# Index work of a graph layer by blocks of 96 edge tiles, early feature loads, and ten gather buffers for twelve

## The chip, the cores and the metric

One core of a Trainium2 chip. The metric is the device time of one execution in microseconds, the median of the runs shown; the profile is of one execution more, with its own time. TensorE is called PE, VectorE DVE, ScalarE ACT, GpSimd POOL; SP issues transfers only.

## What is computed

One message-passing layer on a graph of N = 12,500 nodes with 160 features (64 scalars and 32 vectors of three) and 400,000 edges sorted by destination:

```
h   = relu(layernorm(x))
y0  = h[:, :64] @ W_l1_0 * attr / 8          y1 = (32 vectors of h) x W_l1_1 * attr / sqrt(32)
w   = silu(e16 @ fc_W1 / 4) @ fc_W2 / 8      # 192 weights for each edge
mid = products of w, of y0[src], y1[src] and of the four numbers e4 of the edge   # 96 + 3 x 96
z   = segment sum of mid over dst / sqrt(10)
out = x + sin(pi/8) * (h x W_sc) * attr + cos(pi/8) * (z x W_l2) * attr
```

All in float32. The sum over destinations is a matmul with a selection matrix: 128 edges at a time, a one-hot matrix of the destination inside a window of 32 nodes.

## The kernel before

**Edges.** The 400,000 edges are 3,125 tiles of 128. Four tiles are a batch (782 batches), three tiles a window (`WT`) of at most 32 destination nodes, four windows (12 tiles, three batches) a group (261 groups), eight groups a block of 96 tiles (24 batches; `EG * TG`), 33 blocks.

**Node stage** (lines 268 to 412). The 98 node tiles, and 40 further tiles of rows that are gathered in advance, go through DVE (statistics, centering: L326 to L328), PE (transposes L347 and L348, linear maps L363 and L364), ACT (out of PSUM: L354, L375) and back to DRAM: `y_d` holds the mapped features of all nodes (L378), `yr_d` those of ten batches of edges (L380), called "made" batches: batch 12, 24, ... 120. For these POOL gathers 40 tiles of `x` and 40 columns of `attr` (L306, L309) early on. DVE also adds the skip path into `acc` (L386). After the 16th of the node stage's steps `first_nodes` converts `dst` to float in `drel` (L131), takes the least node of each window (`neg`, L134), and POOL reduces that over the partitions into `negb` (L138).

**`relate`** (L143 to L183) makes the index work on all edges at once: the node tile of each group (`first`, `tile_i`), the places of its four windows (`at`), the limits of each window (`lim`), then over all 3,125 columns: `drel` minus the window's first node (L174), whether an edge falls outside (`over`, L175), whether any does (`far`, L177, then a matmul and `far_i`, L183), and `drel` pushed out of range for these (L179). Such edges would be worked off in a slow loop at the end, which runs zero or one times after `far_i`.

**Edge stage** (L438 to L655). For each batch, `load` (L466 to L475) brings the edge features `xe` by SP, once for eight batches, and the rows of `y_d` by four indirect gathers on POOL into one of the buffers of pool `yg` (L475); a made batch comes from `yr_d` with one transfer on SP (L472). `e4_load` (L515) brings the four numbers of each edge for a block into `raw`, `e4_join` (L522, L523) puts them beside `drel` into `ev` on ACT. `hidden` and `activate` (L484, L489) are the first layer of the edge network, `weigh` (L506) the second, `scale` (L423, L424) multiplies by `e4` and appends the indices, `select` (L537, L539) and `products` (L429 to L436) make the operands on DVE, `sums` (L557 to L564) multiplies and takes the window's sums out, `turn`, `linear`, `add`, `accumulate` (L572 to L604) map a group and add it into `acc`.

**What sets the order.** On PE, ACT and DVE the order inside each `manual_schedule` is written out by hand; between such blocks, and on SP and POOL, a scheduler places instructions, and each engine then works its queue in order. Memory comes from pools: a tile of a later pool waits until the tiles that lie in its place are done with. `load(b + AHEAD)` stands `AHEAD` = 10 batches ahead in the written order; the pool `yg` has 12 buffers, and a gather into a buffer waits for the `products` that read it before. `xe` and `raw` belong to pool `ld`, opened after `relate`.

Of the kernel before, what the change touches and what calls it, by code (L numbers as in the profile page):

```python
# [10 lines left out]
F32 = mybir.dt.float32  # L11
I32 = mybir.dt.int32
AF = mybir.ActivationFunctionType
ALU = mybir.AluOpType
AX = mybir.AxisListType
PSUM = bass.MemoryType.PSUM
DRAM = bass.MemoryType.DRAM

P = 128
# [11 lines left out]
WT = 3  # L31
GW = 4
TG = WT * GW
EG = 8
# [11 lines left out]
def kernel(  # L46
# [19 lines left out]
    nc = tc.nc  # L66
    N = x.shape[0]
    NT = attr.shape[1]
    TP = src.shape[1]
    T = n_edges // P  # L70
    assert n_edges % P == 0 and TP % BT == 0 and NT == (N + P - 1) // P and NT >= 2
    NWIN = (T + WT - 1) // WT
    NG = (NWIN + GW - 1) // GW
    NB = (T + GT - 1) // GT
    ZR = (NT + 1) * P
# [8 lines left out]
    const = ctx.enter_context(tc.tile_pool(name="const", bufs=1))  # L84
# [31 lines left out]
    drel = const.tile([P, TP], F32, name="drel")  # L116
# [2 lines left out]
    far_i = const.tile([1, 1], I32, name="far_i")  # L119
    full = T // WT  # L120

    ygp = ctx.enter_context(tc.tile_pool(name="yg", bufs=12))
    before = ctx.enter_context(ExitStack())
    ip = before.enter_context(tc.tile_pool(name="idx", bufs=1))
    dst_i = ip.tile([P, TP], I32, name="dst_i")
    neg = ip.tile([P, NG * GW], F32, name="neg")
    negb = ip.tile([P, NG * GW], F32, name="negb")

    def first_nodes():

# [6 lines left out]
            nc.vector.tensor_reduce(neg[:, full:NWIN], drel[:, full * WT:T], AX.X, ALU.min, negate=True)  # L137
        nc.gpsimd.partition_all_reduce(negb, neg, P, bass_isa.ReduceOp.max)  # L138

    def relate(rp, cnt):  # L140

        first = rp.tile([P, NG], F32, name="first")
        nc.vector.tensor_reduce(first, negb.rearrange("p (g w) -> p g w", w=GW), AX.X, ALU.max, negate=True)  # L143
        nc.vector.tensor_copy(tile_i, first)
        nc.vector.tensor_scalar(tile_i, tile_i, 7, None, ALU.arith_shift_right)
        nc.vector.tensor_copy(first, tile_i)
        nc.vector.tensor_scalar(first, first, float(NT - 2), None, ALU.min)
        for lo, i in FLOORS:
            nc.vector.tensor_scalar(first[:, lo:], first[:, lo:], float(i), None, ALU.max)
        nc.vector.tensor_copy(tile_i, first)  # L150

        nc.vector.tensor_scalar(first, first, -float(P), None, ALU.mult)
        off = rp.tile([P, NG * GW], F32, name="off")
        nc.vector.tensor_tensor(off.rearrange("p (g w) -> p g w", w=GW),
                                first.unsqueeze(2).to_broadcast([P, NG, GW]),
                                negb.rearrange("p (g w) -> p g w", w=GW), ALU.subtract)
        node_of = rp.tile([P, 1], F32, name="node_of")
        for w in range(GW):
            nc.vector.tensor_scalar(node_of[WN * w:WN * (w + 1), :], lane[WN * w:WN * (w + 1), :],
                                    -float(WN * w), None, ALU.add)  # L160
        for w in range(GW):
            r = slice(WN * w, WN * (w + 1))
            nc.vector.tensor_scalar(at[r, :], off[r, :].rearrange("p (g w) -> p w g", w=GW)[:, w, :],
                                    node_of[r, :], None, ALU.add)
        lim = rp.tile([P, NG * GW], F32, name="lim")
        nc.vector.tensor_scalar(lim, off, -1.0, float(2 * P), ALU.mult, ALU.add)
        nc.vector.tensor_scalar(lim, lim, float(WN), None, ALU.min)
        nc.vector.scalar_tensor_tensor(lim, off, 0.0, lim, op0=ALU.is_ge, op1=ALU.mult)
        over = rp.tile([P, TP], F32, name="over")
        for lo, n, t in ((0, full, WT), (full, NWIN - full, T - full * WT)):  # L170
            if n:
                v = drel[:, lo * WT:lo * WT + n * t].rearrange("p (s t) -> p s t", t=t)
                o = over[:, lo * WT:lo * WT + n * t].rearrange("p (s t) -> p s t", t=t)
                nc.vector.tensor_tensor(v, v, negb[:, lo:lo + n].unsqueeze(2).to_broadcast([P, n, t]), ALU.add)  # L174
                nc.vector.tensor_tensor(o, v, lim[:, lo:lo + n].unsqueeze(2).to_broadcast([P, n, t]), ALU.is_ge)  # L175
        far = rp.tile([P, 1], F32, name="far")
        nc.vector.tensor_reduce(far, over[:, :T], AX.X, ALU.max)  # L177

        nc.vector.scalar_tensor_tensor(drel[:, :T], over[:, :T], float(ZR), drel[:, :T], op0=ALU.mult, op1=ALU.add)  # L179
        if T < TP:  # L180
            nc.vector.memset(drel[:, T:], 0.0)
        nc.tensor.matmul(cnt, far, one, start=True, stop=True)
        nc.vector.tensor_scalar(far_i, cnt, 1.0, None, ALU.min)  # L183

# [48 lines left out]
    def edge_weights():  # L233
        nc.vector.tensor_scalar(w2, w2, 1.0 / math.sqrt(FC_H), None, ALU.mult)
        f = C_X / math.sqrt(10.0 * (M0 + M1))
        nc.vector.tensor_scalar(wc, wor, f, None, ALU.mult)
        nc.vector.tensor_scalar(wc[M0:M0 + M1, 0, 0:M0], wc[M0:M0 + M1, 0, 0:M0], 1.0 / math.sqrt(3.0), None, ALU.mult)
        nc.vector.tensor_scalar(wo[:, :, 0:M0], wor[:, :, 0:M0], f, None, ALU.mult)
        nc.vector.tensor_scalar(wo[M0:M0 + M1, 0, 0:M0], wo[M0:M0 + M1, 0, 0:M0], 1.0 / math.sqrt(3.0), None, ALU.mult)
        nc.vector.tensor_scalar(wo[:, :, M0:].rearrange("p k (u c) -> p k c u", c=3),  # L240
                                wor[:, :, M0:].rearrange("p k (c u) -> p k c u", c=3), f, None, ALU.mult)
# [27 lines left out]
    with (  # L269
# [119 lines left out]
        with tc.manual_schedule(engines=engines):  # L389
# [14 lines left out]
            for q in range(len(steps) + 5):  # L404
# [4 lines left out]
                for stage, lag in ((scales, 1), (leave, 4), (out_of_psum, 2), (turn_rows, 1), (map_rows, 3), (center, 0),  # L409
                                   (add_s, 5)):  # L410
                    if 0 <= q - lag <= last:
                        stage(q - lag)
    with tc.tile_pool(name="rel", bufs=1) as rp, tc.tile_pool(name="rel_p", bufs=1, space=PSUM) as rpp:
        with tc.manual_schedule(engines=engines):
            edge_weights()
            relate(rp, rpp.tile([1, 1], F32, name="cnt"))
    before.close()


    def scale(pw, ev, n):  # L420
# [17 lines left out]
    with (  # L438
        tc.tile_pool(name="selp", bufs=3) as selp,
        tc.tile_pool(name="prod", bufs=3) as prod,  # L440
        tc.tile_pool(name="ld", bufs=2) as ld,
        tc.tile_pool(name="ev", bufs=2) as evp,
        tc.tile_pool(name="hid", bufs=4) as hid,
        tc.tile_pool(name="post", bufs=2) as post,
# [47 lines left out]
        def hidden_pair(s):  # L492

            pair = [i for i in (s, s + 1) if 2 * i < NB]
            for i, ph in [(i, hidden(i)) for i in pair]:
                activate(i, ph)
# [13 lines left out]
        def e4_load(q):  # L510

            if q * EG < NG and q not in ev4:
                lo, hi = q * EG * TG, min((q + 1) * EG * TG, TP)
                raw = ld.tile([P, EG * TG, 4], F32, name="raw")
                nc.sync.dma_start(raw[:, :hi - lo, :].rearrange("p t c -> p (t c)"), e4[:, lo * 4:hi * 4])  # L515
                ev = evp.tile([P, EG * TG, 5], F32, name="ev")
                ev4[q] = ev, raw, lo, hi - lo

        def e4_join(q):
            if q in ev4:  # L520
                ev, raw, lo, n = ev4[q]
                nc.scalar.activation(ev[:, :n, 0:4], raw[:, :n, :], AF.Copy)  # L522
                nc.scalar.activation(ev[:, :n, 4:5], drel[:, lo:lo + n].unsqueeze(2), AF.Copy)  # L523
# [87 lines left out]
                    store(FLOORS[k - 1][1] if k else 0, i)  # L611


        AHEAD = 10
        K = TG // GT
        order = tc.manual_schedule(engines={mybir.EngineType.PE, mybir.EngineType.Activation, mybir.EngineType.DVE})
        with order:
            for b in range(min(AHEAD, NB)):
                load(b)
            e4_load(0)  # L620
            e4_join(0)
            hidden_pair(0)
            weigh(0)
            if NB > 1:
                weigh(1)
            select(0)
            products(0)
            for b in range(NB):
                g, k = divmod(b, K)
                if b + AHEAD < NB:  # L630
                    load(b + AHEAD)
                q, r = divmod(b, EG * K)
                if r == 0:
                    e4_load(q + 1)
                if r == EG * K - 4:
                    e4_join(q + 1)
                if b + 2 < NB:
                    weigh(b + 2)
                if g:
                    (turn, linear, add)[k](g - 1)  # L640
                if b + 1 < NB:
                    select(b + 1)
                    products(b + 1)
                if g and k == K - 1:
                    accumulate(g - 1)
                    leave_before(g)
                sums(b)
                if b % 4 == 0 and b + 4 < NB:
                    hidden_pair((b + 4) // 2)
            for h in ([NG - 2] if NG > 1 else []) + [NG - 1]:  # L650
                for k, stage in enumerate((turn, linear, add, accumulate)):
                    if h == NG - 1 or min(k, K - 1) > (NB - 1) % K:
                        stage(h)
                        if k == 3:
                            leave_before(h + 1)  # L655
# [138 lines left out]
```

## Time and profile before

| what | value |
|---|---|
| three runs | 4033.68, 4042.76, 4043.74 us (median 4042.76) |
| the profiled execution | 4041.36 us, its span 4039.5 us |
| busy: PE, DVE, ACT, POOL | 3237.9 (80%), 2921.0 (72%), 2690.3 (67%), 3021.9 us (75%) |
| gathers L475 on POOL | 3085, mean 950 ns |
| waits of DVE for gathered rows (L429) | 951.5 us in 670 waits |
| granted PE clock, mean | 0.93 |
| `relate` on DVE | 168.87 to 193.16 us |
| first and last gather L475 start | 138.49 and 4018.76 us |

A line of a timeline gives start, duration, engine, source line, operation, output and inputs, how many instructions are merged, and in brackets how long the engine had been idle and what released it. A line of the waits gives the waiting engine and line, what it waited for, the total, the number of waits and the longest. A line of the costliest groups ends with busy time, mean duration of one in ns, and the engine's idle time before these instructions. All times are microseconds from the start of the span unless marked ns.

### The profile page before, as it was taken

The numbers are of one execution on the slowest core, as the hardware profiler recorded it, in microseconds if no ns is written. First come the engines' busy times: TensorE is split into PE (matmuls) and PEld (weight loads), VectorE is DVE, ScalarE is ACT, GpSimd is POOL, SyncE is SP. The second block draws the span as 40 slices with busy tenths as digits, with TensorE's granted clock in tenths as the row PEclk, the third lists the DMA queues.
The fourth block names the chain that finished last, engine by engine and source line by source line (L and its number), as shares of the span: only waits on it lengthen the run. The fifth ranks groups of instructions, "written<-read, shape, count | busy, mean of one in ns | idle before, by whom it ended". The sixth has DMA issues, their size and how long they took to land.

```text
span 4039.5 us, 62548 instructions
## 1 busy us (share of the span) xinstructions
PE 3237.9 (80%) x17505; PEld 2352.5 (58%) x17505; DVE 2921.0 (72%) x7558; ACT 2690.3 (67%) x9543; POOL 3021.9 (75%) x3177
## 2 busy tenths in 40 slices
PE   6689888878787887887777877887787777778887
PEld 5567666555555555555555555555555555555555
DVE  7889777777776776777776777777777767777776
ACT  5488677766666666666666666666666666666665
POOL 7667777777777777777777777777777777777776
PEclk9899999999999899999999999999999999999898
DMA  6333333222232223232223232323233222343232
GB/s 194 107 82 89 80 80 82 74 74 76 74 76 74 74 73 76 74 76 74 74 73 77 74 76 74 76 71 77 74 76 77 74 74 74 76 123 76 71 83 77
DMA packets 244949, 326.49 MB, mean 81 GB/s; under 512 B 67290, under 2 KB 194342, under 8 KB 244342
## 3 DMA queue, kind: packets, MB, share of 16 engines
q0 software_dynamic: 151280, 256.22, 25.6%
q1 hardware_dynamic: 74322, 54.52, 4.7%
q10 hardware_dynamic: 18996, 11.72, 0.9%
q8 instruction: 141, 2.31, 0.2%
q14 instruction: 210, 1.72, 0.1%
HBM read 302.92 MB, written 19.28 MB: 80 GB/s over the span
## 4 chain that ended last, share of the span: by engine, by line
DVE 23%; POOL 22%; issue 20%; DMA 20%; PE 7%; ACT 2%; DVEq 1%; ACTq 0%; POOLq 0%
POOL yg L475 22%; DMA yg<-y_d,src_sb 20%; DVE tmp L431 5%; DVE tmp L429 4%; PE pz L557 3%; DVE pr L434 3%; DVE pr L433 2%; DVE acc L604 2%; DVE sel L539 2%; DVE pr L436 2%; PE pw L506 2%; DVE pr L432 1%; DVE sel L537 1%; PE px L484 1%; ACT pw L423 1%
## 5 line engine op out<-in xcount | busy, mean ns | idle before, releaser
L475 POOL DMA_INDIRECT yg<-y_d,src_sb x3085 | 2929.8, 950 | 958.0 <-issue 749.9
L557 PE MATMUL pz<-pr,sel 128*128 128x256 f32 x6250 | 1628.1, 407 | 0.6 <-DVE pr L436 0.6
L423 ACT ACTIVATE pw<-pw,ev 128x96 f32<-128x96 f32 x3125 | 985.3, 315 | 839.9 <-PE pw L506 750.7
L557 PEld LDWEIGHTS pz<-pr,sel 128*128 128x128 f32 x6250 | 1239.5, 208 | 159.3 <-issue 0.9
L506 PE MATMUL pw<-w,hT 64*128 64x192 f32 x6250 | 761.3, 364 | 649.9 <-DVE pr L436 639.6
L506 PEld LDWEIGHTS pw<-w,hT 64*128 64x128 f32 x6250 | 516.5, 195 | 1043.1 <-DVE pr L436 874.0
L429 DVE TENSOR_TENSOR tmp<-yg,pw 128x384 f32<-128x384 f32 x782 | 432.2, 553 | 952.2 <-DMA yg<-y_d,src_sb 951.5
L564 ACT ACTIVATE zs<-pz 32x64 f32<-32x64 f32 x3126 | 669.8, 214 | 41.7
L431 DVE TENSOR_REDUCE tmp<-tmp 128x128 f32<-128x384 f32 x782 | 463.6, 593 | 27.0
L539 DVE TENSOR_TENSOR sel<-sel,pw 128x384 f32<-128x384 f32 x782 | 432.7, 553 | 26.9
L562 ACT ACTIVATE zs<-pz 32x192 f32<-32x192 f32 x1042 | 337.8, 324 | 155.4 <-PE pz L557 134.3
L434 DVE TENSOR_TENSOR pr<-pw,yg 128x384 f32<-128x384 f32 x782 | 427.0, 546 | 0.0
L484 PE MATMUL px<-xe,w 32*128 32x512 f32 x782 | 293.5, 656 | 73.2 <-issue 65.5
L489 ACT ACTIVATE hT<-px 128x512 f32<-128x512 f32 x391 | 217.7, 595 | 169.3 <-PE px L484 162.5
L432 DVE TENSOR_TENSOR pr<-pw,yg 128x256 f32<-128x256 f32 x782 | 323.4, 414 | 0.0
L433 DVE TENSOR_TENSOR pr<-pw,yg 128x256 f32<-128x256 f32 x782 | 322.6, 413 | 0.0
L537 DVE TENSOR_TENSOR sel<-iota,pw 128x128 f32<-128x128 f32 x782 | 216.5, 277 | 58.4 <-ACT pw L424 57.3
L581 PE MATMUL px<-wc,za 128*128 128x96 f32 (+1 forms) x1566 | 256.4, 304 | 0.4 <-ACT za L574 0.4
L581 PEld LDWEIGHTS px<-wc,za 128*128 128x128 f32 x1566 | 211.2, 205 | 62.7 <-issue 45.5
L595 PE MATMUL px<-os,place 128*128 128x160 f32 x1044 | 221.2, 336 | 0.5 <-ACT os L584 0.5
L436 DVE TENSOR_TENSOR pr<-pw,tmp 128x128 f32<-128x128 f32 x782 | 217.9, 279 | 0.0
L604 DVE SCALAR_TENSOR_TENSOR acc<-px,a_sb,acc 128x160 f32 x522 | 197.6, 379 | 12.6 <-PE px L595 3.3
(97 smaller groups left out, 1747.5 us busy)
## 6 DMA issues: line engine op xcount, KB each, us to landing
yg<-y_d,src_sb POOLq DMA_INDIRECT x3085
xe<-in_e SPq DMA_DIRECT2D x784, 32.0 KB
y_d<-ys ACTq DMA_DIRECT2D x12, 640.0 KB
acc<-in_x SPq DMA_DIRECT2D x11, 640.0 KB
out<-acc SPq DMA_DIRECT2D x11, 640.0 KB
raw<-in_e SPq DMA_DIRECT2D x32, 192.0 KB
yr_d<-ys ACTq DMA_DIRECT2D x5, 640.0 KB
yg<-yr_d SPq DMA_DIRECT2D x10, 320.0 KB
```

Of the source, the lines that this page charges most:

```text
L423: nc.scalar.activation(pw[:, k, 0:96], pw[:, k, 0:96], AF.Copy, scale=ev[:, k, 0:1])
L429: nc.vector.tensor_tensor(tmp[:, :n, 0:3, :], y1, wt[:, :n, NW:NW + 3].unsqueeze(3).to_broadcast([P, n, 3, M1]), ALU.mult)
L431: nc.vector.tensor_reduce(tmp[:, :n, 3, :], tmp[:, :n, 0:3, :].rearrange("p t c u -> p t u c"), AX.X, ALU.add)
L432: nc.vector.tensor_mul(pr[:, :n, 192:PC], wt[:, :n, 96:160], yg[:, :n, 0:M0])
L433: nc.vector.tensor_mul(pr[:, :n, 0:M0], wt[:, :n, 0:M0], yg[:, :n, 0:M0])
L434: nc.vector.tensor_mul(pr[:, :n, 96:192].rearrange("p t (c u) -> p t c u", c=3), wt[:, :n, M0:96].unsqueeze(2).to_broadcast([P, n, 3, M1]) ...
L475: nc.gpsimd.indirect_dma_start(out=yg[:, k, :], out_offset=None, in_=y_d, in_offset=bass.IndirectOffsetOnAxis(ap=src_sb[:, t:t + 1], axis=0))
L506: nc.tensor.matmul(pw[:, k, 0:NW], hT[r, o:o + P], w2[r, :], start=True, stop=True)
L539: nc.vector.tensor_tensor(sel[:, :, 0:3, :], sel[:, :, 3:4, :].to_broadcast([P, n, 3, WN]), wt[:, :n, NW:NW + 3].unsqueeze(3).to_broadcast ...
L557: nc.tensor.matmul(pz[:, 0:PC], sels[g][:, t % TG, :, :], pr[:, k, :], start=t % WT == 0, stop=last)
L564: nc.scalar.activation(zs[:, 192 + M0 * c:192 + M0 * (c + 1)], pz[WN * c:WN * (c + 1), 192:PC], AF.Copy)
L581: nc.tensor.matmul(po[:m, lo:hi], za[:, k, :m], wc[:, k, lo:hi], start=k == 0, stop=k == 1)
```

## The change

Four things. `relate` is cut in two: the part on windows stays (up to `lim`), and the part on edges becomes `relate_edges(q)`, called for block 0 ahead of the edge stage and for block q + 1 at eight batches before the end of block q; `any_far` counts once at the end. The pool `ld` (so `xe` and `raw`) and the tiles `negb`, `fars` and `far` are opened before the node stage's memory; `lim` has a pool `keep` of its own. Pool `yg` has 10 buffers for 12, and `AHEAD` is 9 for 10. `e4_load(0)` comes before the first loads, and `hidden_pair(0)` before `e4_join(0)`.

```diff
@@ -119,12 +119,17 @@
     far_i = const.tile([1, 1], I32, name="far_i")
     full = T // WT
 
-    ygp = ctx.enter_context(tc.tile_pool(name="yg", bufs=12))
+    ygp = ctx.enter_context(tc.tile_pool(name="yg", bufs=10))
+
+    ld = ctx.enter_context(tc.tile_pool(name="ld", bufs=2))
+    NQ = -(-NG // EG)
+    negb = const.tile([P, NG * GW], F32, name="negb")
+    fars = const.tile([P, NQ], F32, name="fars")
+    far = const.tile([P, 1], F32, name="far")
     before = ctx.enter_context(ExitStack())
     ip = before.enter_context(tc.tile_pool(name="idx", bufs=1))
     dst_i = ip.tile([P, TP], I32, name="dst_i")
     neg = ip.tile([P, NG * GW], F32, name="neg")
-    negb = ip.tile([P, NG * GW], F32, name="negb")
 
     def first_nodes():
 
@@ -137,7 +142,7 @@
             nc.vector.tensor_reduce(neg[:, full:NWIN], drel[:, full * WT:T], AX.X, ALU.min, negate=True)
         nc.gpsimd.partition_all_reduce(negb, neg, P, bass_isa.ReduceOp.max)
 
-    def relate(rp, cnt):
+    def relate(rp, lim):
 
         first = rp.tile([P, NG], F32, name="first")
         nc.vector.tensor_reduce(first, negb.rearrange("p (g w) -> p g w", w=GW), AX.X, ALU.max, negate=True)
@@ -162,23 +167,31 @@
             r = slice(WN * w, WN * (w + 1))
             nc.vector.tensor_scalar(at[r, :], off[r, :].rearrange("p (g w) -> p w g", w=GW)[:, w, :],
                                     node_of[r, :], None, ALU.add)
-        lim = rp.tile([P, NG * GW], F32, name="lim")
         nc.vector.tensor_scalar(lim, off, -1.0, float(2 * P), ALU.mult, ALU.add)
         nc.vector.tensor_scalar(lim, lim, float(WN), None, ALU.min)
         nc.vector.scalar_tensor_tensor(lim, off, 0.0, lim, op0=ALU.is_ge, op1=ALU.mult)
-        over = rp.tile([P, TP], F32, name="over")
-        for lo, n, t in ((0, full, WT), (full, NWIN - full, T - full * WT)):
-            if n:
-                v = drel[:, lo * WT:lo * WT + n * t].rearrange("p (s t) -> p s t", t=t)
-                o = over[:, lo * WT:lo * WT + n * t].rearrange("p (s t) -> p s t", t=t)
-                nc.vector.tensor_tensor(v, v, negb[:, lo:lo + n].unsqueeze(2).to_broadcast([P, n, t]), ALU.add)
-                nc.vector.tensor_tensor(o, v, lim[:, lo:lo + n].unsqueeze(2).to_broadcast([P, n, t]), ALU.is_ge)
-        far = rp.tile([P, 1], F32, name="far")
-        nc.vector.tensor_reduce(far, over[:, :T], AX.X, ALU.max)
-
-        nc.vector.scalar_tensor_tensor(drel[:, :T], over[:, :T], float(ZR), drel[:, :T], op0=ALU.mult, op1=ALU.add)
         if T < TP:
             nc.vector.memset(drel[:, T:], 0.0)
+
+    def relate_edges(q, evp, lim):
+
+        lo, hi = q * EG * TG, min((q + 1) * EG * TG, T)
+        over = evp.tile([P, EG * TG], F32, name="over")
+        whole = min(hi // WT, full)
+        for w, n, t in ((lo // WT, whole - lo // WT, WT), (full, (NWIN - full) * (hi == T), T - full * WT)):
+            if n:
+                v = drel[:, w * WT:w * WT + n * t].rearrange("p (s t) -> p s t", t=t)
+                o = over[:, w * WT - lo:w * WT - lo + n * t].rearrange("p (s t) -> p s t", t=t)
+                nc.vector.tensor_tensor(v, v, negb[:, w:w + n].unsqueeze(2).to_broadcast([P, n, t]), ALU.add)
+                nc.vector.tensor_tensor(o, v, lim[:, w:w + n].unsqueeze(2).to_broadcast([P, n, t]), ALU.is_ge)
+        nc.vector.tensor_reduce(fars[:, q:q + 1], over[:, :hi - lo], AX.X, ALU.max)
+
+        nc.vector.scalar_tensor_tensor(drel[:, lo:hi], over[:, :hi - lo], float(ZR), drel[:, lo:hi],
+                                       op0=ALU.mult, op1=ALU.add)
+
+    def any_far(cnt):
+
+        nc.vector.tensor_reduce(far, fars, AX.X, ALU.max)
         nc.tensor.matmul(cnt, far, one, start=True, stop=True)
         nc.vector.tensor_scalar(far_i, cnt, 1.0, None, ALU.min)
 
@@ -410,11 +423,14 @@
                                    (add_s, 5)):
                     if 0 <= q - lag <= last:
                         stage(q - lag)
-    with tc.tile_pool(name="rel", bufs=1) as rp, tc.tile_pool(name="rel_p", bufs=1, space=PSUM) as rpp:
+    with tc.manual_schedule(engines=engines):
+        edge_weights()
+    before.close()
+    keep = ctx.enter_context(tc.tile_pool(name="keep", bufs=1))
+    lim = keep.tile([P, NG * GW], F32, name="lim")
+    with tc.tile_pool(name="rel", bufs=1) as rp:
         with tc.manual_schedule(engines=engines):
-            edge_weights()
-            relate(rp, rpp.tile([1, 1], F32, name="cnt"))
-    before.close()
+            relate(rp, lim)
 
 
     def scale(pw, ev, n):
@@ -438,7 +454,6 @@
     with (
         tc.tile_pool(name="selp", bufs=3) as selp,
         tc.tile_pool(name="prod", bufs=3) as prod,
-        tc.tile_pool(name="ld", bufs=2) as ld,
         tc.tile_pool(name="ev", bufs=2) as evp,
         tc.tile_pool(name="hid", bufs=4) as hid,
         tc.tile_pool(name="post", bufs=2) as post,
@@ -611,15 +626,18 @@
                     store(FLOORS[k - 1][1] if k else 0, i)
 
 
-        AHEAD = 10
+        AHEAD = 9
         K = TG // GT
         order = tc.manual_schedule(engines={mybir.EngineType.PE, mybir.EngineType.Activation, mybir.EngineType.DVE})
         with order:
+            e4_load(0)
             for b in range(min(AHEAD, NB)):
                 load(b)
-            e4_load(0)
+            relate_edges(0, evp, lim)
+            hidden_pair(0)
             e4_join(0)
-            hidden_pair(0)
+            if NQ == 1:
+                any_far(p_x.tile([1, 1], F32, name="px"))
             weigh(0)
             if NB > 1:
                 weigh(1)
@@ -632,8 +650,12 @@
                 q, r = divmod(b, EG * K)
                 if r == 0:
                     e4_load(q + 1)
+                if r == EG * K - 8 and q + 1 < NQ:
+                    relate_edges(q + 1, evp, lim)
                 if r == EG * K - 4:
                     e4_join(q + 1)
+                    if q + 2 == NQ:
+                        any_far(p_x.tile([1, 1], F32, name="px"))
                 if b + 2 < NB:
                     weigh(b + 2)
                 if g:
```

## Prediction

> **What bounds the kernel now.** I read the page first, then the waits of POOL, then the timelines of POOL and DVE from 60 to 235 us, and last the built order of instructions of both kernels. The page:
>
> ```profile
> span 4039.5 us, 62548 instructions
> ...
> POOL yg L475 22%; DMA yg<-y_d,src_sb 20%; DVE tmp L431 5%; DVE tmp L429 4%; PE pz L557 3%; DVE pr L434 3%; DVE pr L433 2%; DVE acc L604 2%; DVE sel L539 2%; DVE pr L436 2%; PE pw L506 2%; DVE pr L432 1%; DVE sel L537 1%; PE px L484 1%; ACT pw L423 1%
> ...
> L475 POOL DMA_INDIRECT yg<-y_d,src_sb x3085 | 2929.8, 950 | 958.0 <-issue 749.9
> ```
>
> No engine looks full (POOL 75%), but the gathers of L475 head the chain. One takes 0.95 us and the next starts 0.30 us later whatever else happens, so POOL spends 1.2525 us on each and 3085 x 1.2525 = 3864 us on all. How little else it waits for, in the waits of POOL:
>
> ```profile
> POOL yg L475 <- issue: 749.9, 2460, 0.3
> ...
> POOL yg L475 <- DVE pr L436: 17.7, 21, 11.7
> ```
>
> The third number is the longest single wait: after its first gather POOL had one real wait, 11.7 us. So the end is the start of the first gather, plus 3864 us, plus what delays POOL, plus a tail. In POOL's timeline:
>
> ```profile
> 120.86 0.98 POOL L309 DMA_INDIRECT ar<-in_attr,ai  x1 [0.31 <-issue]
> 128.61 3.33 POOL L138 PARTITION_ALL_REDUCE negb<-neg  x1 [6.77 <-DVE st L326]
> 138.49 1.19 POOL L475 DMA_INDIRECT yg<-y_d,src_sb  x1 [6.56 <-DMA y_d<-ys]
> ...
> 180.42 3.03 POOL L475 DMA_INDIRECT yg<-y_d,src_sb  x1 [0.30 <-issue]
> ...
> 204.28 0.94 POOL L475 DMA_INDIRECT yg<-y_d,src_sb  x1 [0.30 <-issue]
> 216.88 0.95 POOL L475 DMA_INDIRECT yg<-y_d,src_sb  x1 [11.65 <-DVE pr L436]
> ```
>
> The first gather starts at 138.49, when the last `y_d` store has landed; 48 gathers (12 batches, one for each `yg` buffer) run to 205.2; then POOL stands until `products` frees a buffer. The last gather ends at 4019.71. Check: 138.49 + 3864 + 11.35 (the wait beyond the usual 0.30) + 6.3 (three slow gathers, at 180.42, 183.76 and 190.95) = 4020.1. The tail of 19.8 us is the last batches and stores.
>
> DVE at two places:
>
> ```profile
> 66.59 0.32 DVE L326 BATCH_NORM_STATS2 st<-acc 128x6 f32<-128x160 f32 x1
> 66.94 0.18 DVE L327 BATCH_NORM_AGGREGATE mv<-st 128x2 f32<-128x6 f32 x1
> ...
> 168.87 1.24 DVE L143 TENSOR_REDUCE first<-negb 128x261 f32<-128x1044 f32 x1
> ...
> 179.22 3.40 DVE L174 TENSOR_TENSOR drel<-drel,negb 128x3123 f32<-128x3123 f32 x1
> 182.66 3.41 DVE L175 TENSOR_TENSOR over<-drel,lim 128x3123 f32<-128x3123 f32 x1
> ```
>
> Between them DVE runs the node stage with hardly a gap (53.7 busy us in the 60 from 67 to 127). `relate` starts at 168.87, long after `negb` was there (128.61 + 3.33 = 131.9).
>
> **What the change takes from POOL.** The full-width lines L174, L175, L177 and L179 leave the path. The gathers beside L174, L175 and L179 took 3.03, 3.13 and 3.01 us instead of 0.95: 6.3 us back. The 11.35 us wait goes too, if compute starts soon enough. On the old clock: ACT is done with the node stage at 173.1. The features and `e4` are already in (their loads stand behind the weight loads on SP, about 56 us, not behind `relate` at 193.2), so what remains is the table load 1.28, two Silu 1.09, the join 0.8, the matmuls of `weigh` and their issue about 0.5, scale 1.55 and `products` with `select` 3.3 us: batch 0 is done near 181.7. One block of index work (four operations of about 0.25 us) is done by DVE before ACT needs it.
>
> With 10 buffers POOL stops after 40 gathers: 138.49 + 40 x 1.2525 + 0.24 = 188.8, 7 us after 181.7. The tightest later place is batch 13 (batch 12 comes ready-made through SP and uses a buffer, but no gather): gathers due at 198.9, `products(3)` at 181.7 + 12.1 = 193.8 (`pr` L436 in the trace: 213.33 to 225.39), 5 us of slack. After that compute needs 3.6 us a batch against 5.01 of gathering, and the slack grows. So fewer buffers cost nothing here; 5 us less cover and they would. `AHEAD` itself binds nothing on POOL, since 12 batches ran ahead with a lead of ten. Sum of the gains: 11.35 + 6.3 = 17.7 us.
>
> **What it puts on the path.** The smaller `relate` fits into the node stage's time, and the built order shows it there: on DVE `first<-negb` (L143) is the 166th instruction, where it was the 488th, right behind the batch statistics that start at 66.59. Everything before it is unchanged. POOL's order is unchanged: 40 `xr` and 40 `ar` gathers, then the all-reduce, then `yg`. So DVE comes to `first` at 66.9 us and must wait for `negb`, the last thing POOL makes before the `yg` gathers. DVE takes its queue in order; behind the wait stand the statistics and centering of all further node tiles, hence their transposes on PE, evictions on ACT, the `y_d` stores, and the first gather.
>
> The wait, step by step. POOL's last `ar` gather ended at 121.84. Six gathers after 66.9 took 1.97 instead of 0.96, each beside the 1.47 us addition L386; with DVE standing they do not meet, so 121.84 - 6.1 = 115.8. Then the 6.77 us before the all-reduce, which begin with two POOL configuration instructions at 122.1 and belong to POOL, and 3.33 us: `negb` at 125.9. Wait: 125.9 - 66.9 = 59.0 us (65 if the slow gathers stay).
>
> Then `relate` up to `lim` runs in between: 168.87 to 179.22 = 10.35 us when alone. Woven among other work it is cheaper, since it fills waits between dependent instructions: the weight scaling L236 to L240, 1.62 us of operations, lengthened its three tiles by 1.16 us. That factor, 0.71, gives 7.4; the upper end is 10.35. I take 8.6, as these operations are longer and hide less. Against it: beside the all-reduce L328 took 1.98 and 0.83 instead of 0.30 us, which held up the last `y_d` rows by about 2.2 us and no longer happens: -2.0 (0 to -2.2). First gather: 138.49 + 59.0 + 8.6 - 2.0 = 204.1, which is 65.6 us later. The rest of the node stage and the start of compute move with it, so the slack above holds.
>
> In the edge stage 32 blocks are worked off beside the gathers, each with three DVE operations that read two SBUF tensors. No row of before has such short ones there. The trace shows that a gather that meets one waits until it ends (180.42 + 3.03 is 0.8 after L174's end), while the gather at 187.19, beside the one-input L177, took 0.94. Bounds: 0, and 32 x 3 x 0.25 = 24 us, every operation holding a gather for its whole length. By chance a gather meets a 0.25 us operation in a fifth of cases and for half of it: 96 x 0.2 x 0.125 = 2.4 us, which I take; the long rows above are the same kind, but a short one ends before most gathers need the port.
>
> The Trainium skill, SBUF — State Buffer, section "SBUF: two separate sides", speaks against the change here: the port pair that VectorE and GpSimd share is locked for a whole instruction and the loser fully blocks. Read as every block operation blocking a gather throughout, it makes the sum 4113; by the chance above the sum is 4092.
>
> The rest costs nothing. DVE's 1 us per block lies under its waits for gathers (L429: 951.5 us in 670 waits). The count moves to about batch 764, under the same cover. SP reads it after its last loads, where it now waits 77.9 us anyway. The tail stays.
>
> **Sum.** 65.6 - 17.7 + 2.4 = +50.3 us on the profiled execution's 4041.36 us (span 4039.5 and 1.9 around it): 4091.7. That execution is 1.4 below the median of 4042.76, within the spread of the runs (4034 to 4044); I forecast 4092.
>
> **Rivals.** *DVE does not wait, and the gains stand alone*: the all-reduce is served before DVE needs it. For it: `neg` is ready at 50.5, and POOL could serve it between gathers. Against: 80 gathers stand in front and the trace has it at 128.61. Price: 4041.36 - 17.7 + 2.4 and `relate`'s 8.6 in front of `y_d` = 4034.7, which is within 0.3% (12 us, about what a measurement of this kernel can tell from no change); where the 8.6 hide in the gaps of the node stage too, 4026. The sign changes where `negb` lands at about 76 us, 50 before my figure. 4% for the first, 2% for the second.
>
> *Ten buffers are too few*: compute starts over 5 us later than I put it, or the first batches are slower, and the old wait comes back in part: up to 11 us, 4103. For it: PE starts cold (granted clock 0.53 between 172 and 205). Against: 5 to 7 us of slack. 14%.
>
> *The block operations hold the gathers up*: 21.6 us more, 4113. 5%.
>
> **How the numbers follow.** The forecast has 75%: the wait 59 to 65, weaving 7.4 to 10.4, all-reduce relief 0 to 2.2 and blocks 0 to 8 give 4088 to 4107. The range goes 9 us below that, as the lowest run of before lies 9 below its median, and at the top takes in the second rival with the blocks' 8: 4079 to 4111. Faster 0.02, same 0.04, slower 0.94.
>
> **What would show it.** In the changed profile DVE should wait about 59 us for POOL's `negb` at `first`, from 67 us; the all-reduce should start near 122.6; the first `yg` gather near 204; no gather should wait over 1 us for `pr`; and gathers should stay at 0.95 us. It is wrong if DVE's wait is short, or the first gather starts before 160 us, or POOL waits again later on.

## The result and the profile after

The changed kernel takes 4089.7 us (median of four runs, 4089.34 to 4089.97); the kernel before took 4042.69 beside it. The ratio is 1.0118 (95% interval 1.0105 to 1.013): 47 us slower, against a forecast of 4092. The profiled execution has a span of 4088.2 us and a time of 4089.97, granted PE clock 0.926. Later runs come in groups, each with the kernel before on the same chip; three of those chips ran the kernel before in 5781, 5950 and 5785 us instead of 4034 to 4043, and every number from them is marked as from a slow chip.

The page first. The same group heads it:

```profile
span 4088.2 us, 62698 instructions
...
POOL yg L490 24%; DMA yg<-y_d,src_sb 20%; DVE tmp L447 4%; DVE tmp L445 4%; DVE pr L450 3%; DVE pr L449 2%; PE pz L572 2%; DVE sel L554 2%; DVE acc L619 2%; DVE pr L452 2%; PE pw L521 1%; DVE pr L448 1%; DVE sel L552 1%; PE px L499 1%; DVE place L602 1%
...
L490 POOL DMA_INDIRECT yg<-y_d,src_sb x3085 | 2926.9, 949 | 1016.4 <-issue 729.0
```

The gathers cost POOL what they did (2926.9 us busy against 2929.8), and POOL is idle 58 us longer ahead of them. Where, the waits of POOL and of DVE say:

```profile
POOL yg L490 <- DMA y_d<-ys: 76.1, 1, 76.1
...
POOL yg L490 <- DVE pr L452: 12.5, 41, 0.3
```

```profile
DVE first L148 <- POOL negb L143: 59.9, 1, 59.9
```

One wait of 76.1 us for the `y_d` store has come; the 11.7 us wait for `products` has gone (longest now 0.3). Behind the first stands DVE's single wait for `negb`. The timelines of DVE and POOL around it:

```profile
64.96 0.32 DVE L339 BATCH_NORM_STATS2 st<-acc 128x6 f32<-128x160 f32 x1
125.15 1.24 DVE L148 TENSOR_REDUCE first<-negb 128x261 f32<-128x1044 f32 x1 [59.86 <-POOL negb L143]
...
126.39 0.23 DVE L185 TENSOR_TENSOR drel<-drel,negb 128x96 f32<-128x96 f32 x1
```

```profile
115.01 0.94 POOL L322 DMA_INDIRECT ar<-in_attr,ai  x1 [0.30 <-issue]
121.78 3.33 POOL L143 PARTITION_ALL_REDUCE negb<-neg  x1 [5.83 <-issue]
201.20 1.19 POOL L490 DMA_INDIRECT yg<-y_d,src_sb  x1 [76.09 <-DMA y_d<-ys]
```

From 65.3 to 125.15 DVE does nothing, and the engines behind it in the node stage stand as well. The table by stretches (columns: busy time of PE, PE's weight loads, DVE, ACT and POOL with instruction counts, then granted clock, DMA share, GB/s):

```profile
0.00:65.00 65.00, 40.70 (x236) 33.51 (x236) 48.06 (x165) 31.80 (x64) 43.83 (x51) 0.92 0.80 252
65.00:125.00 60.00, 0.24 (x2) 0.00 (x0) 0.29 (x2) 1.27 (x3) 41.97 (x42) 0.53 0.13 34
125.00:201.00 76.00, 59.68 (x383) 50.03 (x383) 67.69 (x240) 46.13 (x99) 0.11 (x1) 0.92 0.23 72
```

POOL works on its `xr` and `ar` gathers in the middle stretch; everybody else waits for it. In the third it is POOL that waits.

### The profile page after: what moved, and what is told of

The parts are those of the page before. It is cut to its first block, busy times and chain, and to the rows that moved or that the text cites. A ratio compares the mean times of both kernels' runs of the same rounds, so it can differ in the third digit from the quotient of the medians.

```text
span 4088.2 us, 62698 instructions
## 1 busy us (share of the span) xinstructions
PE 3241.7 (79%) x17505; PEld 2356.5 (58%) x17505; DVE 2930.9 (72%) x7687; ACT 2690.6 (66%) x9543; POOL 3012.9 (74%) x3177
## 4 chain that ended last, share of the span: by engine, by line
POOL 24%; DVE 22%; issue 21%; DMA 21%; PE 5%; ACT 1%; DVEq 1%; POOLq 0%; ACTq 0%
POOL yg L490 24%; DMA yg<-y_d,src_sb 20%; DVE tmp L447 4%; DVE tmp L445 4%; DVE pr L450 3%; DVE pr L449 2%; PE pz L572 2%; DVE sel L554 2%; DVE acc L619 2%; DVE pr L452 2%; PE pw L521 1%; DVE pr L448 1%; DVE sel L552 1%; PE px L499 1%; DVE place L602 1%
## 5 line engine op out<-in xcount | busy, mean ns | idle before, releaser
L490 POOL DMA_INDIRECT yg<-y_d,src_sb x3085 | 2926.9, 949 | 1016.4 <-issue 729.0
L552 DVE TENSOR_TENSOR sel<-iota,pw 128x128 f32<-128x128 f32 x782 | 217.9, 279 | 50.6 <-ACT pw L440 50.3
```

Source lines behind the costliest of these rows:

```text
L490: nc.gpsimd.indirect_dma_start(out=yg[:, k, :], out_offset=None, in_=y_d, in_offset=bass.IndirectOffsetOnAxis(ap=src_sb[:, t:t + 1], axis=0))
```

## The experiments

**The theory**: DVE takes its queue in order, the first operations that need `negb` stand among the node stage's work, and so the first gather and with it the end come about 60 us late; the rest of the change is worth 17 us or so to the good. **Rivals**: the new memory places or the ten buffers make the loss; or the block operations hold up the gathers.

**The kernel after again, and two ways to take the wait away.** All three ran on one chip, where the kernel before took 4034.01 us. The first run is the kernel after as it is:

> The kernel after itself, unchanged, as the yardstick of the two runs beside it, since the earlier runs of the edited kernels fell on chips where the kernel before took 5781 and 5950 us and the kernel after was not among them. Theory (VectorE is held at the block operation `first` until the all-reduce of `negb` is done, and the node stage and the first gather with it): where the kernel before takes about 4043 us this one takes 4090, the wait of `first` for `negb` is about 60 us and the first gather stands at about 201. Where the kernel before takes 5700 us or more, GpSimd waits for VectorE's products through the whole edge stage and is not what the end is counted from; the wait must still be there, 50 us or more. Rival (the memory placement or the lead of nine batches makes the loss): the wait may be shorter, and the kernel is no slower than the one that holds the block operations back.

Measured: 4080.34 us, ratio 1.0114 (1.0097 to 1.0131); the first gather at 200.89, DVE's wait 59.8. The same loss on a chip on which both kernels are 9 us quicker.

The second run holds `relate` back to the end of the node stage's order on DVE. `first` and `off` lie in `dst_i`, which is free by then, so that no memory has to wait:

```diff
+        first = dst_i[:, NG * GW:NG * GW + NG].bitcast(F32)
+        off = dst_i[:, 0:NG * GW].bitcast(F32)
...
                     if 0 <= q - lag <= last:
                         stage(q - lag)
+            relate(ip, lim)
...
-    with tc.tile_pool(name="rel", bufs=1) as rp:
-        with tc.manual_schedule(engines=engines):
-            relate(rp, lim)
```

> The kernel after with the first block's operations held back until the node stage is written out on VectorE; all else as in the kernel after. Theory: no wait of VectorE for `negb` ahead of the node stage; where the kernel before takes about 4043 us, 4025 (4090 less the wait of 60 and the weaving, and with about 5 us given back): faster than the kernel after by 55 to 70 us, and than the kernel before by 10 to 25. Where the kernel before takes 5700 or more, faster than the kernel after by 10 to 60 us, since the start of the edge stage still counts in full but less of the early time is spent on that wait alone. Rival: within 10 us of the kernel after.

Measured: 4076.07 us, ratio 1.0103 (1.0086 to 1.012); 4 us won where 55 to 70 were expected. By the time alone the theory would have fallen. The timeline of DVE in this run shows why it need not:

```profile
65.94 1.52 DVE L400 TENSOR_TENSOR acc<-acc,ys 128x1280 f32<-128x1280 f32 x1
67.38 0.32 DVE L340 BATCH_NORM_STATS2 st<-acc 128x6 f32<-128x160 f32 x1
126.46 0.26 DVE L186 TENSOR_TENSOR drel<-drel,negb 128x96 f32<-128x96 f32 x1 [58.76 <-POOL negb L144]
126.63 0.18 DVE L341 BATCH_NORM_AGGREGATE mv<-st 128x2 f32<-128x6 f32 x1
```

The wait is still there, at another instruction. `drel` of block 0, the first operation of `relate_edges(0)`, reads only `drel` and `negb`; it belongs to no hand-written order, and the scheduler put it in front of the same statistics. A 0.26 us operation of the edge stage holds the node stage for 58.8 us. The edit had not taken away what it was meant to.

The third run leaves all operations of the change where they are and makes `negb` early instead: POOL's order is written out too, twelve of the 40 tiles are gathered, then comes the all-reduce, then the other 28:

```diff
-        with tc.manual_schedule(engines=engines):
+        with tc.manual_schedule(engines=engines | {mybir.EngineType.Pool}):
...
-                    gather_x()
+                    gather_x(0, min(12, RT))
                 if q == min(16, mid):
                     first_nodes()
+                    gather_x(12, RT)
```

> The kernel after with the index order of the first batches made on twelve tiles alone, so that the all-reduce of `negb` comes early on GpSimd and the first block is not held. Theory: the all-reduce ends at about 75 us, VectorE does not wait for it by more than 10 us, the first gather is earlier than in the kernel after by 40 us or more where the kernel before takes 4043, and the time is about 4036 there. Where the kernel before takes 5700 or more: within 25 us of the kernel that holds the block operations back, and faster than the kernel after. Rival: no faster than the kernel after.

Measured: 4028.28 us (4028.1 to 4030.84), ratio to the kernel before 0.9988 (0.9978 to 0.9997): 52 us faster than the kernel after on the same chip, by an edit that touches POOL's order alone. The expected 4036 was for a chip with 4043 and is 4027 here; the all-reduce was to end at about 75 us and ends at 61.66. POOL's timeline, and the wait that is left on DVE:

```profile
58.33 3.33 POOL L143 PARTITION_ALL_REDUCE negb<-neg  x1 [5.86 <-issue]
...
149.50 0.94 POOL L500 DMA_INDIRECT yg<-y_d,src_sb  x1 [7.84 <-DMA y_d<-ys]
```

```profile
DVE drel L185 <- POOL negb L143: 7.5, 1, 7.5
```

The all-reduce starts 64 us earlier and the first gather 51.4 us. It is still 11 us later than in the kernel before: the hand-written order on POOL lets it stand 7.0 us for its first `ar` gather, and DVE still waits 7.5 us. Memory places, buffers, lead and block operations are those of the kernel after in the program text, so none of them makes the loss.

**All block operations held.** To the second run's kernel one operation is added, so that `drel` cannot go ahead either:

```diff
+        nc.vector.tensor_scalar(negb, negb, 0.0, None, ALU.add)
         nc.vector.tensor_scalar(lim, off, -1.0, float(2 * P), ALU.mult, ALU.add)
```

> The run that held back `first` alone was 4 us faster than the kernel after, not 65: its waits show VectorE held 58.8 us at `drel` of the first block, which the scheduler of the edge stage had put among the node stage's work, for the same `negb`. Here `drel` is held as well: the tables' operations, now last in the node stage's order, write `negb` over itself once (a sum with zero, about 0.7 us), so that no block operation can stand ahead of them. Theory: no wait of VectorE for `negb` over 1 us; the first gather at 137 (196.1 - 58.8) or 138 and the time, where the kernel before takes 4034, 4076 - 59 = 4017, with up to 8 us more for VectorE's 15 us of table work beside the first gathers: 4015 to 4027, faster than the kernel before by 7 to 20. Rival (the node stage is late for another reason, and the wait only shows it): the first gather stays past 180 and the time within 15 us of 4076. Where the kernel before takes 5700 or more, the run tells only whether the wait is gone.

Measured: 4029.33 us (4027.39 to 4032.24) where the kernel before took 4042.92: ratio 0.9967 (0.9954 to 0.9979), 13.6 us faster than before. The expectation named 4015 to 4027 for a chip with 4034, which is 4024 to 4036 here. DVE's waits no longer name `negb`; POOL's timeline:

```profile
127.50 3.33 POOL L144 PARTITION_ALL_REDUCE negb<-lim  x1 [5.94 <-DVE mv L342]
139.38 1.19 POOL L488 DMA_INDIRECT yg<-y_d,src_sb  x1 [8.56 <-DMA y_d<-ys]
...
172.19 1.91 POOL L488 DMA_INDIRECT yg<-y_d,src_sb  x1 [0.30 <-issue]
...
176.97 1.12 POOL L488 DMA_INDIRECT yg<-y_d,src_sb  x1 [0.30 <-issue]
178.39 1.68 POOL L488 DMA_INDIRECT yg<-y_d,src_sb  x1 [0.30 <-issue]
```

The first gather is back at 139.38, within 0.9 us of the kernel before, although the all-reduce stands nearly where it stood (128.61 before): nothing on DVE asks for it until 168. This version beats both kernels. What it gains is most of what the forecast gave to the change without its wait: the wait for `products` is gone (11.35) and the three slow gathers cost 1.9 us together instead of 6.3. Less the 0.9 us of the first gather these make 14.9 us; the span is 11.4 us shorter than that of the kernel before (4028.1 against 4039.5), since each of the 3,084 steps from gather to gather is about 1.1 ns longer, 3.5 us in all.

**The same edits and others on slow chips.** Eight runs fell on the slow chips. There the kernel is not bound by POOL: in the kernel with `relate` held back POOL waits 1634 us for `products`, and PE's granted clock is 0.77. The chain of waits of one of them (the kernel with late loads, below) puts 53% on PE and 21% on "another core or an unknown queue", in pieces of up to about 10 us. The node stage, too, is late by itself, so that DVE comes to `negb` when it is ready. What decides on a normal chip is therefore not tried here, and the ratios say little.

> The changed kernel with one thing undone: the window part of the index work stands at the end of the node stage's written order on DVE, so that nothing of it can be woven in ahead (its tables lie in tiles that are free by then). Theory (DVE's wait for negb and the woven work put off the first gather by 62.7 us, and the end follows it one for one): DVE waits for negb no more, first gather back near 137 us, time 4089.7 - 64 = 4025 us, with up to 5 us more if ten buffers are just too few. Rival A (the cost lies in the edge stage: ten buffers, or index work beside the gathers): time stays near 4089. Rival B (the early feature loads disturb the node stage): first gather stays late, 4089.

> The changed kernel, with POOL's order in the node stage written out: 12 of the 40 row gathers (and as many attr gathers), then the reduction that makes negb, then the rest. The weaving stays. Theory: negb is there near 58 us, DVE waits about 5 us where it comes to it, the woven work costs its 7 us still, first gather near 148 us, time near 4036 us. If it is not the place of the reduction in POOL's queue that matters: no change, 4089. If the weaving itself were the larger cost: little gain, over 4070.

> The changed kernel with one thing undone: the window part of the index work stands at the end of the node stage's written order on DVE, so that nothing of it can be woven in ahead. (The first look fell on a chip where the kernel of before itself took 5781 us at a granted clock of 0.77, with POOL waiting for compute 1634 us, so that POOL bound nothing there.) Theory, on a chip where before takes 4043: DVE waits for negb no more, first gather back near 137 us, 4025 us, with up to 5 us more if ten buffers are just too few. Rival A (the cost lies in the edge stage: ten buffers, or index work beside the gathers): near 4089. Rival B (the early feature loads disturb the node stage): first gather stays late, 4089.

> The changed kernel, with POOL's order in the node stage written out: 12 of the 40 row gathers (and as many attr gathers), then the reduction that makes negb, then the rest. The weaving stays. Theory, on a chip where before takes 4043: DVE waits about 5 us where it comes to negb, the woven work costs its 7 us still, first gather near 148 us, 4036 us. If the place of the reduction in POOL's queue did not matter: 4089. If the weaving itself were the larger cost: over 4070.

Measured on the first slow chip (kernel before 5781.42): `relate` held 5749.87, ratio 0.9949 (0.9914 to 0.9984), first gather at 231.46; all-reduce early 5734.86, ratio 0.9926 (0.989 to 0.9962), first gather at 219.07. On the second (before 5949.72): 5918.35, 0.9948 (0.9925 to 0.9972), and 5900.45, 0.9925 (0.9891 to 0.9959). The hidden flaw of the first edit does not show here: no DVE wait for `negb` in either of its two traces.

A further one put `relate` in the middle of the node stage (at its step 36, where DVE was expected at about 96 us on a normal chip, some 32 us before `negb`):

```diff
+                if q == 36:
+                    relate(ip, lim)
```

> Dose: as e1_hold, but the window part stands in the written order at step 36 of the node stage, where DVE of the changed kernel would come at about 96 us. Theory: wait for negb about 32 us (POOL's last gather is slowed by three additions more, negb near 128), 10.4 us of index work, first gather near 177 us, time 4065 us. A threshold effect instead of a one-for-one shift would give 4025 or 4089.

Measured: 5752.55, ratio 0.9947 (0.9916 to 0.9978), no wait for `negb`, first gather at 243.19. Inconclusive: `negb` was ready 43 us before `relate` came to it. On a normal chip it was not tried.

The lead by itself, the kernel before with ten buffers and nine batches:

```diff
-    ygp = ctx.enter_context(tc.tile_pool(name="yg", bufs=12))
+    ygp = ctx.enter_context(tc.tile_pool(name="yg", bufs=10))
...
-        AHEAD = 10
+        AHEAD = 9
```

> The kernel before with 10 buffers and a lead of nine, and nothing else. Theory: POOL stops after 40 gathers instead of 48 and batch 13 waits for products of batch 3 (225.7 us) instead of batch 1 (216.9): 8 to 9 us more, 4051 us; no other wait of POOL later. Rival (a lead of nine or ten buffers is enough anywhere): no change, 4042. Rival (ten buffers cost all along the edge stage): over 4070.

> The kernel before with ten buffers for gathered rows instead of twelve and a lead of nine batches; nothing else changed. Theory (a buffer is a batch of gathers that GpSimd may run ahead, 5.01 us): GpSimd stops after 40 gathers, near 195, and waits until batch 0 is done at 213.6, so its first wait is 20 to 23 us instead of 11.65, and the time is 10 us above the kernel before (8 to 12). Rival (compute is the bound there, so that buffers don't matter, or the lead costs through the whole edge stage): the time within 3 us of the kernel before, or 20 and more above it.

Measured: 5783.43 beside 5781.42, ratio 1.0011 (0.9978 to 1.0043), and on a third slow chip 5784.49 beside 5784.93, ratio 1.0015 (0.9985 to 1.0044). No difference where compute is the bound, as the rival had it for such a case; the price of two buffers on a normal chip stays open.

Last, the version that beats both, with the memory for features and `e4` opened late as in the kernel before:

```diff
-    ld = ctx.enter_context(tc.tile_pool(name="ld", bufs=2))
...
         tc.tile_pool(name="prod", bufs=3) as prod,
+        tc.tile_pool(name="ld", bufs=2) as ld,
```

> The run with all block operations behind the node stage (4029.3 us where the kernel before took 4042.9), with one more thing undone: the memory for features and `e4` is opened after the node stage, as in the kernel before, so their loads wait for the node stage's end. In the kernel before these loads began at 193.2, where `relate` ended, and ScalarE waited 31.5 us for `raw`. Theory (it was `relate`'s own 25 us and its memory that held them, and the early loads matter only for what is left): loads from 173 to 178, the table load near 182 to 186 instead of 177.6, batch 0 done near 190 to 193 instead of 186.3, batch 3 at 203 to 206 against a gather due at 199.7: GpSimd waits 3 to 7 us for a buffer and the time is 3 to 8 us above that run, 4032 to 4037 where the kernel before takes 4043 (9 less where it takes 4034). Rival 1 (the early loads carry the whole of the 27 us by which compute starts sooner): the wait is 15 to 25 us and the time 4044 to 4054. Rival 2 (the loads were never late): no wait over 1 us and the time within 2 us of 4029.

Measured, on the third slow chip: 5753.97, ratio 0.9943 (0.9905 to 0.9981). The time tells nothing, but one wait does. On these chips, too, POOL runs through its ten buffers and then waits for `products` of batch 0, and that wait measures how late compute starts. Timelines of POOL in three kernels with ten buffers: loads early and `relate` small (held), loads late and `relate` small, and the kernel before with ten buffers:

```profile
322.60 0.94 POOL L487 DMA_INDIRECT yg<-y_d,src_sb  x1 [41.14 <-DVE pr L449]
```

```profile
329.16 0.94 POOL L488 DMA_INDIRECT yg<-y_d,src_sb  x1 [44.75 <-DVE pr L449]
```

```profile
350.93 0.94 POOL L475 DMA_INDIRECT yg<-y_d,src_sb  x1 [69.33 <-DVE pr L436]
```

Opening the loads late costs 3.6 us, between two chips (2.6 against 42.18 in the other run of the held kernel); up to 1.9 us of it may be the chip, since the kernel before with ten buffers waits 69.33 us on the third slow chip and 67.47 on the first. The full `relate`, the loads behind its memory and the later `e4` load cost 24.6 us more, on the same chip. On the first slow chip the whole way, from 67.47 to 41.14, is 26.3 us. Normal chips show 28.2: batch 0's `products` ends 75.1 us after the first gather in the kernel before (213.61 less 138.49) and 46.9 us in the version that holds all (186.25 less 139.38). So most of the sooner start comes from no longer waiting for the full `relate` and the memory that it held, and a few us at most from opening the loads early; `relate`'s columns, its memory and the order of the `e4` load were not tried apart. That division is shown on slow chips alone.

## Why the prediction was right

The forecast was 4092 us with 0.94 on slower; 4089.7 came. The mechanism is the one forecast. That the number is within 3 us is in part luck: the first gather came 2.9 us sooner than forecast, and the steps between gathers took 1.3 us more than the term that stood for them, for a reason that the runs do not show. Its steps:

- **DVE waits for `negb`**: 59.0 forecast, 59.86 measured. The steps hold one by one: the last `ar` gather at 115.01 without 1.97 us gathers beside the idle DVE, the all-reduce at 121.78 (122.6 forecast). Of the two runs that take this wait away, the one with the early all-reduce gains 52 us (same chip); the one that holds all ends 13.6 us below the kernel before.
- **`relate` woven into the node stage**: mis-sized. 8.6 us forecast with 7.4 as the low end; 6.8 measured from the end of the wait to the next skip-path addition (125.15 to 138.84, against 66.94 to 73.83 in the kernel before). The run that kept the table work out, on the other chip, puts it at 3.8 at the first gather: 200.89 less 59.8, against 196.07 less 58.8.
- **All-reduce off DVE's path**: -2.0 forecast, -2.3 measured (from that addition to the first gather 62.36 us, 64.66 before; no run tried the all-reduce by itself).
- **First gather**: 204.1 forecast, 201.20 measured. DVE also reached the wait 1.6 us sooner, at 65.3, so 62.7 later = -1.6 + 59.9 + 6.8 - 2.3.
- **Gains on POOL**: 17.7 forecast; the wait (11.35) and the slow gathers (6.3) are both gone.
- **Block operations**: mis-sized. 2.4 us forecast. Setting the timelines of POOL and DVE side by side, 39 gathers met one of 133 block operations and took 0.952 us on average, all others 0.9485: 0.15 us in all. Nearly all of it lies in three gathers of 0.97 to 1.02 us that started while a block operation ran (last section). The estimate had every gather that meets one held; but 62 of the 100 two-input ones began and ended inside a gather and held nothing. In the second execution of the kernel after, 43 gathers met one, for 0.04 us. What looks like the term need not be it: without the three gathers of 3 us they were busy 3.4 us longer than in the kernel before (2926.9 against 2923.5), but in the second execution of the same kernel only 2918.1, so that an execution's chip moves them more than the change.
- **Sum**: 62.7 - 17.7 + 3.7 (gather period after, 1.25366 against 1.25247 us, by 3084) = +48.7 = 4088.2 - 4039.5. The forecast's +50.3 had an error of -2.9 in the first gather and +1.3 in the period. The cause of the 3.7 stays open: the block operations held gathers for 0.15 us; the run that holds all has about the same (3.5), and no run tells the change from the chip here.
- **Ten buffers are enough**: right, by less than forecast. ACT's table load came at 240.74, after a wait of 5.34 us for the last `yr_d` store that the forecast had left out, and batch 0 was done at 249.3 instead of 244.4 (181.7 and the 62.7). Batch 3 ended at 261.13, ahead of a gather due about 261.6: 0.5 us of slack where the text had 5. In the second execution POOL did wait there, 1.53 us, 1.2 more than usual. That is one of the forecast's own signs of being wrong, and the rival "ten buffers are too few" in small:

```profile
262.64 0.95 POOL L490 DMA_INDIRECT yg<-y_d,src_sb  x1 [1.53 <-DVE pr L452]
```

The rival "DVE does not wait" was priced at 4034.7, or 4026 if the table work hides; the version that holds all measures 4029.33. So the price of that case was right; only the built order of instructions decided that it was not this one. "Block operations hold the gathers up" (4113) is refuted by the 0.15 us.

The Trainium skill, SBUF — State Buffer, section "SBUF: two separate sides", was cited against the change: an instruction on the shared port pair keeps the other engine out for its whole length. Read as every block operation holding a gather throughout, it would have made 21.6 us more than the forecast; the measurement decides, and it was 0.15 us in all. The trace agrees with the section for three gathers that started while a block operation ran: they ended 0.82 us after it. It does not agree the other way round: the 62 block operations inside gathers of 0.95 us took at most 0.29 us, against 0.25 on average.

## What to carry to other kernels

In the order of an in-order engine, look for the first instruction that reads something made late by another engine, and for everything queued behind it: one 0.26 us operation cost 59 us here. When an experiment takes such a wait away, read the waits before the time: holding one consumer back only moved the wait to the next, which a scheduler had hoisted, and the time alone would have spoken against a right theory. Making the value early (52 us) and asking for it late (first gather 62 us earlier) are two separate cures, and either was enough to end below the kernel before: by 5.7 us with `negb` early, where part of the wait was left, and by 13.6 with all held.

## What the runs showed of the hardware

A gather on POOL that starts while DVE is in certain operations ends 0.81 to 0.83 us after the end of that operation. An undisturbed one takes 0.95 us, so it loses time only where the operation runs on for over 0.13 us after the gather's start. In the version that holds all, DVE's timeline has two operations of 1.25 us that read two SBUF tensors:

```profile
172.04 1.25 DVE L160 TENSOR_TENSOR dst_i<-dst_i,negb 128x1044 f32<-128x1044 f32 x1
...
178.00 1.25 DVE L174 SCALAR_TENSOR_TENSOR lim<-dst_i,lim 128x1044 f32<-128x1044 f32 x1
```

The gathers that started inside them (172.19 + 1.91 and 178.39 + 1.68) ended 0.81 and 0.82 us after them; in the kernel before the one beside L174 ended 0.83 us after it. A length of 0.25 us is enough, as DVE and POOL of the kernel after show:

```profile
3250.10 0.25 DVE L189 SCALAR_TENSOR_TENSOR drel<-over,drel 128x96 f32<-128x96 f32 x1
```

```profile
3250.15 1.02 POOL L490 DMA_INDIRECT yg<-y_d,src_sb  x1 [0.31 <-DVE over L186]
```

Two further block operations did the same in that trace (gathers at 508.96 and 2648.50, of 0.99 and 0.97 us). Nor does it take two SBUF inputs. The first pair is of the kernel after, where `place` reads one tensor and a column of scalars, and the gather ended 0.82 us after it; the second is of the kernel before, where the gather started 0.07 us ahead of a conversion and ended 0.13 us after it:

```profile
296.81 0.34 DVE L602 TENSOR_SCALAR place<-iota,at 128x256 f32<-128x256 f32 x1
```

```profile
296.92 1.06 POOL L490 DMA_INDIRECT yg<-y_d,src_sb  x1 [0.30 <-DVE pr L452]
```

```profile
44.09 1.78 DVE L131 CAST drel<-dst_i 128x3136 f32<-128x3136 int32 x1
```

```profile
44.02 1.98 POOL L309 DMA_INDIRECT ar<-in_attr,ai  x1 [0.31 <-issue]
```

Reductions held none, long as they are: beside L177 of the kernel before (3.41 us) a gather took 0.94. Neither did the operations of `select` and `products` that read `pw`, of 0.28 to 0.55 us, in the traces of the normal chips. Which property of an operation decides was not tried.

The slow chips were not expected: the same kernel took 43% longer there (5781 against 4034), with waits of up to about 10 us on PE, ACT and DVE for something that the profile cannot name, and a granted clock of 0.77 instead of 0.93. What causes them stays open.
